# Attention beside a mixture of experts: nine attention steps per block instead of eleven, and a rule for which two may share a gap

## The chip, the cores and the metric

The kernel runs on one core of a Trainium2 chip. Its time is the device time of one execution in microseconds (us); smaller is better. The time before is the median of three executions, 1349.92 us (1348.86 to 1350.81).

## What is computed

Both halves read the layer norm of the same input, and their results are added to the input. The input has 8 sequences of 1024 tokens, each token 256 wide; everything is float32.

```python
def attn(x):                                   # 16 heads of 16
    q, k, v = (x @ W.T for W in (Wq, Wk, Wv))  # split into heads
    q, k = elu(q) + 1, elu(k) + 1
    kv_cumsum = cumsum(einsum('blhd,blhe->blhde', k, v), axis=1)
    k_cumsum = cumsum(k, axis=1)
    out = einsum('blhd,blhde->blhe', q, kv_cumsum)
    denom = clip(einsum('blhd,blhd->blh', q, k_cumsum), 1e-6)
    return (out / denom) @ Wo.T

def ffn(x):                                    # 8 experts, best 2 per token
    c = softmax of the two largest of (x @ Wr + br), zero elsewhere
    h = silu(x @ W1[e]) * (x @ W3[e])          # 256 -> 512
    return sum over e of c[e] * (h @ W2[e])    # 512 -> 256

xn = layernorm(x)
return x + attn(xn) + ffn(xn)
```

## The kernel before

**Two kinds of work share the engines.** The experts' part is cut into tiles of 128 tokens that go to one expert: `NM` = 132 tiles, run by the loop over `j` (L1268). One tile is `ffn_step(j)` (L1237): it gathers the tokens of tile j + 3, loads the two weight matrices of tile j + 2 (1 MB, L1182), multiplies tile j by them (`ffn_hidden`, tile `gu_ps`, two PSUM banks, L1199), turns the tokens of tile j + 1 (`ffn_turn`, tile `xg_t`), multiplies the hidden values of tile j - 1 by the third matrix (`ffn_out`, tile `y_ps`, L1218) and stores finished rows by a scattering DMA that adds (`ffn_store`, L1229).

The attention is cut into `NBLK` = 16 blocks of 512 tokens, and a block into `NCH` = 4 chunks of 128. It is linear attention with a causal mask inside a chunk and a running state `kv` across chunks. A block's work comes in these pieces, to which the text gives letters:

- **Q** (L795) and **K** (L811): projections of queries and keys, four matmul groups in all, each into one bank; ScalarE and VectorE then make elu + 1 of them. **T** (L858): the keys are turned. **V** (L811): the projection of values. **D** (L880): denominators; their reciprocals go through memory and come back as `rden` (L892, L898).
- **S**c, `scores(t, c)` (L909): the products of chunk c into **four banks** `s_ps` (L919); VectorE multiplies each bank by the causal mask into `s_sb` (L926). Then the chunk's part of the state, `kv_ps` (L934), which VectorE adds to `kv` (L939, L941).
- **W**c, `weigh` (L945): state times queries (L953) and masked scores times values (L960) into `o_ps`; VectorE multiplies by `rden` into `oT` (L967).
- **A**c, `attend` (L972): `oT` times the output weights into `a_ps` (L979); ScalarE copies it to `at` (L984), and a DMA on GpSimd's queue adds `at` to the output after the fourth chunk (L989; in the last block after each chunk, L987).

**PSUM.** There are eight banks in three pools. Pool `mm` has four: Q, K and V take one for each group, `gu_ps` takes two, and S takes all four. Pool `y` has two (`y_ps`, `a_ps`, `den`), and pool `t` has two (`xg_t`, `kv_ps`, `o_ps` and the turned keys).

**Order.** A Python generator, `block_steps(t)` (L993), yields once per step; a block has 11. Before each tile, the loop calls `attend_upto(n)` (L1021) with a quota n, and that many steps in total are then issued ahead of the tile. The text calls the place between two tiles a gap. From `j` = 22 (`READ`) on, 148 steps are spread over 106 gaps, 1.4 to a gap, so that about four gaps in ten hold two steps, whichever two they happen to be. Up to `j` = 11 a step comes every other gap; from 12 to 21, where VectorE also builds the second list of tokens, two come in each.

After the opening part the order in each engine's queue is not that of the program: a scheduler places instructions by a model of when their operands and buffers will be ready, and takes the earlier in the program where several are. DMAs on SyncE's queue keep the program's order among themselves.

Of the kernel before, what the change touches and what calls it, by code (L numbers as in the profile page):

```python
# [63 lines left out]
def tile_attention_moe(  # L64
# [20 lines left out]
    NCH = TB // P  # L85
    N = B * L
    NBLK = N // TB
# [821 lines left out]
    def scores(t, c):  # L909

        qT, qm, kT, kn, va, rden = blocks[t]
        first = t % BLK_PER_SEQ == 0 and c == 0
        last = t % BLK_PER_SEQ == BLK_PER_SEQ - 1 and c == NCH - 1
        span = bass.ts(c, P)
        s_ps = [ps_mm.tile([P, KC, 2, P], F32, tag="mm", name="s_ps") for r in range(4)]
        for hh in range(KC):
            for r in range(4):
                rows = slice(32 * r, 32 * r + 32)
                nc.tensor.matmul(  # L919
                    s_ps[r][:, hh].rearrange("p a l -> p (a l)"), lhsT=kT[rows, hh, span],  # L920
                    rhs=qm[rows, hh, :, span], start=True, stop=True,
                )
        s_sb = []
        for r in range(4):
            sm = masked.tile([P, KC * 2, P], F32, tag="s_sb", name="s_sb")
            nc.vector.tensor_tensor(  # L926
                sm, s_ps[r].rearrange("p k a l -> p (k a) l"), causal_b, ALU.mult
            )
            s_sb.append(sm)
        before_c = state[0]  # L930
        if not last:
            kv_ps = ps_t.tile([P, KC, P], F32, tag="t", name="kv_ps")
            for hh in range(KC):
                nc.tensor.matmul(  # L934
                    kv_ps[:, hh, :], lhsT=kn[:, c, bass.ts(hh, P)],
                    rhs=own_v(va, c, 4 * hh, 4 * hh + 4), start=True, stop=True,
                )
            new = three.tile([P, KC, P], F32, tag="kv", name="kv")
            nc.vector.tensor_tensor(new, kv_ps, heads_b, ALU.mult)  # L939
            if not first:  # L940
                nc.vector.tensor_tensor(new, new, before_c, ALU.add)  # L941
            state[0] = new
        return t, c, s_sb, before_c
# [28 lines left out]
    def attend(t, c, oT):  # L972
# [17 lines left out]
        if c == NCH - 1:  # L990
            del ats[t], blocks[t]

    def block_steps(t):  # L993

        for i, _ in enumerate(project(t)):
            if i in (1, 3, 5, 8):
                yield
        if t + 1 < NBLK:
            fetch(t + 1)
        waiting = scores(t, 0)  # L1000
        yield
        for c in range(NCH):
            coming = scores(t, c + 1) if c + 1 < NCH else None
            oT = weigh(*waiting)
            yield
            attend(t, c, oT)
            if c in (0, 2):
                yield
            waiting = coming

    STEPS = 11
    steps_made = [0]

    def attention():
        for t in range(NBLK):
            yield from block_steps(t)

    steps = attention()
    copied = []

    def attend_upto(n):  # L1021
        while steps_made[0] < min(n, NBLK * STEPS):
            next(steps)
            steps_made[0] += 1
        if steps_made[0] == NBLK * STEPS:
            next(steps, None)


    EN = mybir.EngineType
    with tc.manual_schedule(engines={EN.DVE, EN.Activation, EN.PE, EN.Pool}):  # L1030
        parts = [moments(t, 1) for t in range(FB)]
        lgT4 = e_one.tile([P, FB, P], F32, name="lgT4")
        small_constants()
        next(parts[0])
        qs = [project_q(0, o) for o in range(KC)]
        for t in range(FB):
            if t + 1 < FB:
                next(parts[t + 1])
            next(parts[t])
            normalise(t)  # L1040
            turn(t)
            if t == 1:
                logits(0, lgT4[:, 0, :])
            elif t == 0:
                xnTs[0] = turned_first.pop()
                begin(0)
            if t < KC:
                next(qs[t])
        last_moments = moments(FB, 1)
        next(last_moments)  # L1050
        for t in range(1, FB):
            logits(t, lgT4[:, t, :])
        for _ in last_moments:
            pass
        lg4 = ps_t.tile([P, FB * P], F32, tag="t", name="lg4")
        for t in range(FB):
            nc.tensor.transpose(lg4[:, bass.ts(t, P)], lgT4[:, t, :], ident)
        store(FB - 1)
        add_logits(0, FB, lg4)
        for q in qs:  # L1060
            next(q)
        normalise(FB)
        ks = [project_k(0, c) for c in range(0, NCH, 2)]
        routing = route(0, FB)
        next(routing)
        next(ks[0])
        next(routing)
        turn(FB)
        next(ks[1])
        for q in qs:  # L1070
            next(q)
        next(routing)
        listing = first_batch()
        next(listing)
        next(routing)
        lg_t = logits_turned(FB)
        vs = [project_v(0, c) for c in range(0, NCH, 2)]
        next(vs[0])
        next(listing)
        next(vs[0])  # L1080
        next(listing)
        add_logits(FB, 1, lg_t)
        next(listing)
        for o in range(KC):
            mask_q(0, o)
        next(vs[1])
        for k in ks:
            next(k)
        for _ in moments(FB + 1, 1):
            pass  # L1090
        next(vs[1])
        attend_upto(3)

        for _ in range(2):
            idle_ps = ps_mm.tile([P, TB], F32, tag="mm", name="idle_ps")
            nc.tensor.matmul(
                idle_ps, lhsT=ident, rhs=blocks[0][0][:, 0, :], start=True, stop=True
            )
        next(routing)

        nc.scalar.activation(warm, ones[:, 0:1], AF.Silu)
# [135 lines left out]
    def ffn_step(j, behind):  # L1237


        if j + 3 < NM:  # L1240
            ffn_load(j + 3)
        if j + 2 < NM:
            ffn_weights(j + 2)
        if j < NM:
            ffn_hidden(j, j == NM - 1)
        if j + 1 < NM:
            ffn_turn(j + 1)
        if j > 0 and j != NM - 1:
            ffn_out(j - 1)
        for _ in range(2):  # L1250
            if stored[0] < j - behind:
                ffn_store(stored[0])
                stored[0] += 1
# [10 lines left out]
    LATE = 3  # L1264
    LISTS = NBLK - FB
    READ = LISTS + 10
    AHEAD = 2 + LISTS // 2 + 2 * (READ - LISTS)
    for j in range(NM + 1):  # L1268
        if j + 1 < NM:
            ffn_norm(j + 1)  # L1270
        t = FB + j
        if FB < t <= NBLK and t % ROUND == 0:
            for _ in routing:
                pass
        if 0 < j and t < NBLK:
            if j % 2 == 0:
                with tc.issue_after(last_token[0].ins):
                    for _ in moments(t, 2):
                        pass
            normalise(t)  # L1280
            turn(t)
            if t + 5 < NBLK:
                load_x(t + 5, nc.scalar)
            add_logits(t, 1, logits_turned(t))
            if (t + 1) % ROUND == 0:
                routing = route(t + 1 - ROUND, t + 1)
                next(routing)
        if j == LISTS:
            in_order(
                nc.sync.dma_start(  # L1290
                    out=tab_d[1][1 : 1 + NS * P, :].rearrange("(p i) w -> p (i w)", p=P),
                    in_=tab.rearrange("p i w -> p (i w)"),
                )
            )
            in_order(nc.sync.dma_start(out=tab_d[1][0:1, :], in_=before[0:1, 0:3]))
            lists = second_batch(taken)
        if LISTS <= j < READ:
            next(lists)
        if LISTS <= j < LISTS + NBLK - FB:
            t = FB + j - LISTS  # L1300
            rows = slice(t * TB, (t + 1) * TB)
            in_order(nc.sync.dma_start(out=out_rows[rows, :], in_=x_rows[rows, :]))
        if j < LISTS:
            attend_upto(3 + j // 2)
        elif j < READ:
            attend_upto(AHEAD - 2 * (READ - j - 1))
        else:
            attend_upto(AHEAD + (NBLK * STEPS - AHEAD) * (j - READ + 1) // (NM - READ - 4))
        if j == N1 + 1:
            copied.append(j)  # L1310
            in_order(nc.sync.dma_start(out=out_rows[0 : FT * P, :], in_=acc_d[:, :]))
        ffn_step(j, LATE if N1 < j <= N1 + LATE else 0)
    while stored[0] < NM:
        ffn_store(stored[0])
        stored[0] += 1
# [50 lines left out]
```

## Time and profile before

| | |
|---|---|
| median of the timed runs | 1349.92 us |
| the profiled execution | 1333.92 us |
| its span, first to last instruction | 1332.0 us |
| TensorE's mean granted clock | 0.992 |
| PE busy | 1279.3 us, 96% |
| PE weight loads busy | 1094.5 us, 82% |
| VectorE, ScalarE, GpSimd busy | 48%, 39%, 40% |
| DMA, over the span | 187 GB/s |

The profiled execution took 16.0 us less than the median of the timed ones. All sums below are made against the profiled execution. Matmuls overlap in the profile: a row's duration runs beyond the start of the next row. How long a group held TensorE is therefore read from its start to the start of the next group. Each float32 matmul stands as two records, so that `gu_ps` has 32 records for a tile.

### The profile page before, as it was taken

To read this page: it belongs to the slowest core of one execution; us is meant where nothing else is said; L and a number is where in the kernel's file an instruction comes from. 1 tells how busy PE (TensorE), PEld (TensorE's weight loads), DVE (VectorE), ACT (ScalarE), POOL (GpSimd) and SP (SyncE) were. 2 spreads that over 40 slices of the span, in tenths; PEclk is the share of its full clock that TensorE was granted. 3 is DMA by queue.
4 is the path that set the end of the run, shared out by engine and by line. 5 is a ranking of instruction groups with operands and counts; after the bars stand their busy time and mean duration, and the time that the engine had idled before them with its cause. 6 is when DMAs were issued, how large, how long until landed. Compare 5 with 4: busy or idle time off the path is not lost.

```text
span 1332.0 us, 28306 instructions
## 1 busy us (share of the span) xinstructions
PE 1279.3 (96%) x10968; PEld 1094.5 (82%) x10968; DVE 635.0 (48%) x1436; ACT 516.5 (39%) x1052; POOL 528.2 (40%) x460
## 2 busy tenths in 40 slices
PE   5799999999999999999999999999999999999996
PEld 4578787878888788888888888888888888888885
DVE  7867498753353425353443535253533534252531
ACT  4666373531515142342516152432425151524321
POOL 3634433333334334344344434344344343343432
PEclk9999999999999999999999999999999999999998
DMA  9898756566776667576666766675766676576663
GB/s 339 276 297 238 201 162 180 127 179 174 205 201 169 173 142 204 134 195 166 151 188 144 201 164 178 160 195 146 176 165 150 176 175 183 144 198 148 179 163 76
DMA packets 163462, 240.36 MB, mean 180 GB/s; under 512 B 16098, under 2 KB 87394, under 8 KB 163042
## 3 DMA queue, kind: packets, MB, share of 16 engines
q1 hardware_dynamic: 119938, 184.31, 44.4%
q0 software_dynamic: 38064, 43.22, 20.1%
q10 hardware_dynamic: 5328, 11.01, 2.3%
q8 instruction: 90, 1.47, 0.4%
q14 instruction: 42, 0.34, 0.1%
HBM read 196.30 MB, written 52.67 MB: 187 GB/s over the span
## 4 chain that ended last, share of the span: by engine, by line
PE 86%; DVE 8%; DMA 3%; SPq 1%; issue 1%; ACT 1%; POOL 0%; POOLq 0%; DVEq 0%; ACTq 0%
PE gu_ps L1199 35%; PE y_ps L1218 16%; PE s_ps L919 6%; PE o_ps L960 4%; PE a_ps L979 4%; PE zq L795 4%; PE zkk L811 4%; PE zkv L811 3%; PE xg_t L1166 2%; PE kv_ps L934 2%; DVE s_sb L926 2%; PE o_ps L953 2%; DMA xb<-in_x_dram 2%; DVE ksum L863 1%; DMA acc_d<-in_x_dram 1%
## 5 line engine op out<-in xcount | busy, mean ns | idle before, releaser
L1199 PE MATMUL gu_ps<-xgT,w 128*128 128x128 f32 x4224 | 512.4, 278 | 4.6 <-DVE s_sb L926 2.8
L1199 PEld LDWEIGHTS gu_ps<-xgT,w 128*128 128x128 f32 x4224 | 492.3, 192 | 29.4 <-issue 15.7
L1145 POOL DMA_INDIRECT xg<-in_x_dram,src_i x132 | 131.9, 999 | 451.9 <-ACT xgT L1168 361.2
L1218 PE MATMUL y_ps<-w_sb,hT 128*128 x1056 | 251.8, 381 | 2.8 <-DVE hT L1210 2.5
L1229 POOL DMA_INDIRECT out_dram<-y,dst_i x107 | 173.8, 1624 | 164.8 <-DVE y L1225 71.5
L1210 DVE TENSOR_TENSOR hT<-gu_ps,hT 128x512 f32<-128x512 f32 x132 | 91.1, 690 | 272.0 <-PE gu_ps L1199 254.5
L1218 PEld LDWEIGHTS y_ps<-w_sb,hT 128*128 128x128 f32 x1056 | 190.7, 191 | 25.5 <-DVE hT L1210 2.7
L1207 ACT ACTIVATE hT<-gu_ps 128x512 f32<-128x512 f32 x132 | 78.8, 597 | 334.9 <-PE gu_ps L1199 332.7
L926 DVE TENSOR_TENSOR s_sb<-s_ps,causal 128x512 f32<-128x512 f32 x256 | 162.7, 682 | 52.6 <-PE s_ps L919 49.8
L1225 DVE TENSOR_SCALAR y<-y_ps,entry 128x256 f32<-128x256 f32 x132 | 63.6, 482 | 145.3 <-PE y_ps L1218 145.2
L1150 POOL DMA_INDIRECT entry<-tab_d,of_i x107 | 110.0, 1028 | 36.8 <-issue 31.7
L1168 ACT COPY xgT<-xg_t 128x256 f32<-128x256 f32 x132 | 49.1, 372 | 157.8 <-PE xg_t L1166 152.6
L919 PE MATMUL s_ps<-qm,kT 32*128 32x256 f32 x1024 | 95.4, 406 | 1.4 <-DVE hT L1210 0.4
L984 ACT COPY at<-a_ps 128x256 f32<-128x256 f32 x64 | 23.8, 371 | 170.7 <-PE a_ps L979 170.7
L919 PEld LDWEIGHTS s_ps<-qm,kT 32*128 32x128 f32 x1024 | 55.9, 183 | 31.2 <-issue 18.5
L1157 ACT ACTIVATE xg<-xg,entry 128x256 f32<-128x256 f32 x132 | 79.7, 603 | 3.6 <-DVE v L286 3.2
L1229 POOL DMA_INDIRECT acc_d<-y,src_i x25 | 43.5, 1742 | 76.9 <-DVE y L1225 47.4
L979 PE MATMUL a_ps<-wo_sb,oT 128*128 128x256 f32 x256 | 67.6, 386 | 5.6 <-DVE oT L967 5.4
L960 PE MATMUL o_ps<-s_sb,va 128*32 128x128 f32 x2048 | 72.3, 278 | 0.0
L960 PEld LDWEIGHTS o_ps<-s_sb,va 128*32 128x32 f32 x2048 | 53.2, 110 | 9.2 <-issue 0.9
L795 PE MATMUL zq<-xnT,wq_sb 128*128 128x512 f32 x128 | 60.2, 603 | 0.0
L979 PEld LDWEIGHTS a_ps<-wo_sb,oT 128*128 128x128 f32 x256 | 46.2, 190 | 16.8 <-DVE oT L967 9.7
(211 smaller groups left out, 1363.5 us busy)
## 6 DMA issues: line engine op xcount, KB each, us to landing
w<-in_w_dram SPq DMA_DIRECT2D x264, 512.0 KB
den_d<-over SPq DMA_DIRECT2D x64, 128.0 KB
rden<-den_d SPq DMA_DIRECT2D x16, 512.0 KB
xnT_d<-xnT ACTq DMA_DIRECT2D x15, 512.0 KB
xnT<-xnT_d SPq DMA_DIRECT2D x15, 512.0 KB
out_dram<-in_x_dram SPq DMA_DIRECT2D x12, 512.0 KB
out_dram<-at POOLq DMA_DIRECT2D x12, 512.0 KB, 8.2
xb<-in_x_dram SPq DMA_DIRECT2D x10, 512.0 KB
```

What stands on the lines that cost most here:

```text
L795: nc.tensor.matmul(z, lhsT=wq_sb[:, k, bass.ts(o, P)], rhs=xnTs[t][:, k, :], start=(k == 0), stop=(k == KC - 1),)
L811: nc.tensor.matmul(z[:, i, :], lhsT=xnTs[t][:, k, bass.ts(c + i, P)], rhs=wkv_sb[:, k, a, :], start=(k == 0), stop=(k == KC - 1),)
L919: nc.tensor.matmul(s_ps[r][:, hh].rearrange("p a l -> p (a l)"), lhsT=kT[rows, hh, span], rhs=qm[rows, hh, :, span], start=True, stop=True,)
L926: nc.vector.tensor_tensor(sm, s_ps[r].rearrange("p k a l -> p (k a) l"), causal_b, ALU.mult)
L960: nc.tensor.matmul(o_ps[32 * r : 32 * r + 32, hh, :], lhsT=va[:, c, 4 * hh + r, a, :], rhs=s_sb[r][:, 2 * hh + a, :], start=(first and a = ...
L979: nc.tensor.matmul(a_ps, lhsT=oT[:, hh, :], rhs=wo_sb[:, hh, :], start=(hh == 0), stop=(hh == 1),)
L1145: nc.gpsimd.indirect_dma_start(out=xg[j], out_offset=None, in_=x_rows[:, :], in_offset=bass.IndirectOffsetOnAxis(ap=src_i[:, i : i + 1], a ...
L1150: nc.gpsimd.indirect_dma_start(out=entry[j], out_offset=None, in_=table[:, :], in_offset=bass.IndirectOffsetOnAxis(ap=num_i[:, i : i + 1], ...
L1199: done = nc.tensor.matmul(ps[:, i, :], lhsT=w13[:, k, bass.ts(i, P)], rhs=xgT[j][:, k, :], start=(k == 0), stop=(k == KC - 1),)
L1210: nc.vector.tensor_tensor(hT, gu[1], hT, ALU.mult)
L1218: done = nc.tensor.matmul(y_ps, lhsT=hT[:, i, :], rhs=w2_sb[:, bass.ds(e * (IC * H) + i * H, H)], start=(i == 0), stop=(i == IC - 1),)
L1229: nc.gpsimd.indirect_dma_start(out=rows[:, :], out_offset=bass.IndirectOffsetOnAxis(ap=dst_i[:, i : i + 1], axis=0), in_=ys.pop(j), in_off ...
```

## The change

A block now has nine steps. **A**c is no longer a step of its own: it is issued in a later step, behind the next chunk's scores. `attend_upto` gets a rule: a second (or third) step joins a gap only if its number in the block is 0, 4 or 8; otherwise it waits for the next gap, even if the quota is not met. The call in the opening part is exempt.

| step | before | after |
|---|---|---|
| 0 | A3 of the block before, Q | Q, A3 of the block before |
| 1 | K | K |
| 2 | T | T |
| 3 | V, D | V, D |
| 4 | S0 | S0 |
| 5 | S1, W0 | S1, W0 |
| 6 | A0 | S2, A0, W1 |
| 7 | S2, W1 | S3, A1, W2 |
| 8 | A1, S3, W2 | W3, A2 (in the last block A3 too) |
| 9 | A2 | |
| 10 | W3 | |

```diff
+    behind = []
+
     def block_steps(t):
 
+
         for i, _ in enumerate(project(t)):
+            if i == 1 and behind:
+                attend(*behind.pop())
             if i in (1, 3, 5, 8):
                 yield
         if t + 1 < NBLK:
             fetch(t + 1)
         waiting = scores(t, 0)
         yield
+        done = None
         for c in range(NCH):
             coming = scores(t, c + 1) if c + 1 < NCH else None
+            if done and c + 1 < NCH:
+                attend(*done)
             oT = weigh(*waiting)
+            if done and c + 1 == NCH:
+                attend(*done)
+            done = t, c, oT
+            waiting = coming
+            if c + 1 < NCH or t + 1 < NBLK:
+                yield
+        behind.append(done)
+        if t + 1 == NBLK:
+            attend(*behind.pop())
             yield
-            attend(t, c, oT)
-            if c in (0, 2):
-                yield
-            waiting = coming
-
-    STEPS = 11
+
+    STEPS = 9
+
+    TOGETHER = (0, 4, 8)
     steps_made = [0]
...
-    def attend_upto(n):
+    def attend_upto(n, apart=True):
+        first = True
         while steps_made[0] < min(n, NBLK * STEPS):
+            if apart and not first and steps_made[0] % STEPS not in TOGETHER:
+                break
             next(steps)
             steps_made[0] += 1
-        if steps_made[0] == NBLK * STEPS:
-            next(steps, None)
+            first = False
...
-        attend_upto(3)
+        attend_upto(3, False)
...
-    AHEAD = 2 + LISTS // 2 + 2 * (READ - LISTS)
+    AHEAD = 2 + LISTS // 2 + 3 * (READ - LISTS) // 2
...
-            attend_upto(AHEAD - 2 * (READ - j - 1))
+            attend_upto(AHEAD - 3 * (READ - j - 1) // 2)
         else:
             attend_upto(AHEAD + (NBLK * STEPS - AHEAD) * (j - READ + 1) // (NM - READ - 4))
...
+    assert steps_made[0] == NBLK * STEPS
```

`AHEAD` falls from 28 of 176 steps to 23 of 144, and from `j` = 22 on 121 steps are spread over the same 106 gaps.

## The prediction

> **What bounds the kernel now.** I read the page first (busy shares, chain of waits), then the stages, then the timelines of PE and VectorE gap by gap.
>
> ```profile
> PE 1279.3 (96%) x10968; PEld 1094.5 (82%) x10968; DVE 635.0 (48%) x1436; ACT 516.5 (39%) x1052; POOL 528.2 (40%) x460
> ...
> PE 86%; DVE 8%; DMA 3%; SPq 1%; issue 1%; ACT 1%; POOL 0%; POOLq 0%; DVEq 0%; ACTq 0%
> ```
>
> The chain runs through PE for 86% of the span; no other engine is half busy. So the time is PE's work plus the time in which PE waits, and a change of order can win only the second. The stages say where:
>
> ```profile
> 360.00:1289.00 929.00, 921.28 (x7999) 797.17 (x7994) 387.42 (x687) 326.77 (x606) 377.77 (x311) 1.00 0.66 170
> ```
>
> (Columns: window, length, busy PE, weight loads, VectorE, ScalarE, GpSimd, then clock, DMA share, GB/s.) In this long stage PE looks 99% busy, at full clock, with DMA at 0.66. Waits inside a run of matmuls don't show there; the timeline has them. Two gaps, the first with S0 and then S1, W0, the second with S2, W1 (rows: start, length, line, what, records):
>
> ```profile
> 364.16 1.89 PE L1218 MATMUL y_ps<-w_sb,hT 128*128 x8
> 365.98 1.15 PE L919 MATMUL s_ps<-qm,kT 32*128 32x256 f32 x16
> 367.05 0.71 PE L934 MATMUL kv_ps<-va,kn 128*128 128x128 f32 x4
> 367.89 2.92 PE L919 MATMUL s_ps<-qm,kT 32*128 32x256 f32 x16
> 370.74 0.71 PE L934 MATMUL kv_ps<-va,kn 128*128 128x128 f32 x4
> ...
> 384.93 1.15 PE L919 MATMUL s_ps<-qm,kT 32*128 32x256 f32 x16
> 386.01 0.71 PE L934 MATMUL kv_ps<-va,kn 128*128 128x128 f32 x4
> 386.56 0.61 PE L953 MATMUL o_ps<-qT,kv 128*128 128x128 f32 x4
> 387.10 1.08 PE L960 MATMUL o_ps<-s_sb,va 128*32 128x128 f32 x32
> ```
>
> From start to next start, S takes 1.08 us alone (384.93 to 386.01), but 2.85 as the second S of a gap (367.89 to 370.74). VectorE's timeline has the cause: the four masks of the first S take 2.48 us, and each frees one of the four banks that the second S wants.
>
> ```profile
> 367.14 2.48 DVE L926 TENSOR_TENSOR s_sb<-s_ps,causal 128x512 f32<-128x512 f32 x4 [0.57 <-PE s_ps L919]
> ...
> 370.43 1.89 DVE L926 TENSOR_TENSOR s_sb<-s_ps,causal 128x512 f32<-128x512 f32 x3
> 372.23 0.41 DVE L939 TENSOR_TENSOR kv<-kv_ps,heads 128x256 f32<-128x256 f32 x1
> 372.68 0.42 DVE L941 TENSOR_TENSOR kv<-kv 128x256 f32<-128x256 f32 x1
> 373.02 0.68 DVE L926 TENSOR_TENSOR s_sb<-s_ps,causal 128x512 f32<-128x512 f32 x1
> ```
>
> A second kind of wait is an A placed before its `oT` is made:
>
> ```profile
> 601.86 0.71 PE L919 MATMUL s_ps<-qm,kT 32*128 32x256 f32 x6
> 602.83 1.13 PE L979 MATMUL a_ps<-wo_sb,oT 128*128 128x256 f32 x4 [0.27 <-DVE oT L967]
> 603.89 1.12 PE L919 MATMUL s_ps<-qm,kT 32*128 32x256 f32 x10
> ```
>
> **What the Trainium skill says.** (1) "Perfetto Trace Analysis", section Identifying the Most-Contended Engine: matmul busy share is no measure of PE's headroom, because matmuls are pipelined. The trace agrees: 99% busy in a stage whose gaps hold 39 us of waiting (below). (2) The same page, section Matmuls: independent groups should rotate through PSUM banks so that emptying one overlaps the next group. Two S on the same four banks cannot; the trace shows 1.77 us for it. (3) "TensorE: Matmul & The Clock Gate", section Step-by-step: matmuls stay in program order, only weight loads are pulled ahead. So W, A and the tile behind a waiting S wait too; at 367.89 nothing overtakes.
>
> **The price list.** Undisturbed paces, start to next start, from the same timeline: a tile 5.52 us (`gu_ps` 3.57, `xg_t` 0.22, `y_ps` 1.73), S 1.08, kv 0.55, W 1.01 plus 0.54 for its state part, A 0.86, Q 3.43, K and V 3.46, T 0.87, D 0.57. For each of the 100 gaps from 360 to 1295 us I take tile start to tile start less these. The sum is 39.2 us of waiting, by what shares the gap:
>
> - S0 with S1 W0, four gaps, 2.3 each: 9.2
> - S2 W1 with A1 S3 W2, four, 2.0 each: 8.0
> - A0 with S2 W1 where `oT` is late, two at 1.36; A inside the next `gu_ps` before its `oT`, four at 0.4 to 1.0: 5.6
> - T with V D, six at 0.5 to 0.64: 3.6
> - V D with S0, four at 0.49: 2.0. S0 alone, five at 0.53 (the next `gu_ps` needs a bank that is being masked): 2.7
> - the other 77, about 0.1 each: 8.0
>
> **After the change, stage from 360 us.** I ran the new quota and rule by hand over j. In blocks 3 to 15 every gap holds one step, except V D with S0 (8 times), S3 A1 W2 with W3 A2 (5), W3 A2 with Q (2).
>
> - No gap has two S, and none has T with V: 9.2 + 8.0 + 3.6 go.
> - A0 stands behind S2, A1 behind S3, A2 behind W3, A3 behind Q. In the late case above `oT` is done at 602.78, and an S and kv begun at 601.86 last until 603.49, so no wait is left: the 5.6 go.
> - V D with S0: 8 x 0.49 = 3.9. S0 alone 5 x 0.53 = 2.7. V D alone 5 x 0.1 = 0.5.
> - S with W in one gap, 34 gaps outside the pairs, at the 0.17 to 0.30 of today's such gaps, mean 0.22: 7.5. Q 1.4 and W3 A2 1.0 at 0.11; K and T none.
> - S3 A1 W2 with W3 A2: not in the trace. W3 needs the fourth mask of S3, which needs W2's end, because seven `s_sb` buffers serve eight. Nearest row: W ends at 372.84, that mask at 373.70; W3's state part covers 0.54, so 0.3 to 0.4 is left. Bounds: 0 if the scheduler puts W3 into the next `gu_ps`; 1.2 if VectorE makes `oT` and adds `kv` (0.41 + 0.42) first. I take 0.4, and 0.22 as before: 5 x 0.6 = 3.0.
>
> Sum 20.0; 39.2 - 20.0 = 19.2, taken as **18** for the small terms that a scheduler moves.
>
> **Up to 360 us.** To j = 7 nothing changes. From j = 8 to 24 (124 to 360 us) I count 28 us of waiting, much of it behind VectorE, which is 13.46 of 14 us busy in one gap with the token lists. Clear collisions: S1, S2 and S3 close together at 222 to 233 us, 2.8; S0 with S1 W0 at 282 to 295 us, 4.9, in which the clock falls (0.87 in that window; the Trainium skill, "TensorE: Matmul & The Clock Gate", section What's actually happening, ties half clock to an idle window, and PE waits much in this one). Both go. Against that, S2 A0 W1 comes to j = 8, where A0 alone stood, about 1; and j = 18 gets three steps at once (S3 A1 W2, W3 A2, Q), 1 to 2. Bounds: no gain, or 10. I take **5**.
>
> **Edits at nothing.** Q and K never share a gap now, so ScalarE loads its table (1283 ns) up to twice more in some blocks; ScalarE is 39% busy and `gu_ps` covers it with 3.57 us; uncovered, it would be 1.3 a time. A3 comes 3.4 us later, and with it the DMA of `at` on GpSimd's queue and the gather behind it: gathers are three tiles ahead. Once, at j = 26, SyncE's copy from `acc_d` waits for that DMA (8.5 us today) with weight loads behind it; two tiles of weights are ahead, so 3.4 more is covered; uncovered it costs 3.4 once. The assertion and the exemption in the opening issue nothing.
>
> **The end.** In the last block A1, A2 and A3 now come together at j = 127, so three `at` DMAs, not two, go ahead of the last stores on GpSimd, which follow each other at 4.5 to 5.3 us there. One more is some 3 us, of which the tiles take up most: I add **1** (0 to 3).
>
> **Sum.** 18 + 5 - 1 = 22 us of the profiled 1333.92, so about 1312 there. The timed median is 16.0 us higher for a reason that the profile doesn't show; I carry it unchanged: 1349.9 - 22 = **1328**. About 0.2% (2.7 us) is what a measurement of this kernel can tell from no change.
>
> **Rivals.**
> - *The collisions go, the early stage gives nothing or a little back* (1334): VectorE's list work sets the pace from 167 to 282 us, and moved steps just wait elsewhere. Against it: the wait at 282 us has VectorE half idle. 18 - 1 - 1 = 16.
> - *More goes* (1317): early 10, V D with S0 hidden better, no half-clock window; 33 us at most.
> - *The other side: A in the middle of S.* The queue is the scheduler's, not the program's. If it judges `oT` ready midway through S2 and S3, the pattern at 601.86 (1.16 us: 0.57 + 0.20 + 0.39, where S, A and S wait) comes back in up to three gaps of each of 13 blocks: 39 x 1.16 = 45, less 22: 1373. It decides from 19 such gaps of 39 on. For it: the pattern is in the trace. Against: there A came first in the program, and S overtook it; now S comes first.
> - *It doesn't do what it says*: the scheduler moves a step's S into the neighbouring gap, so that two meet again. If half the collisions of S stay, 9 come back: 1337. In the trace S stays within its gap from 360 us on.
>
> **How the numbers follow.** Forecast 0.47; early stage gives nothing 0.14; more goes 0.08; half the collisions stay 0.08; A in the middle, weak (within 2.7 us of no change) 0.06 and decisive 0.17. Hence faster 0.77, same 0.06, slower 0.17. The range 1315 to 1349 takes in the first four cases, with the unknown costs (pairs 0 to 6, early 0 to 10, end 0 to 3), and part of the weak one; about 0.2 lies outside.
>
> **What would show it.** PE's busy time nearly as before; S at 1.08 in every gap after 360 us; no wait of A for `oT`; VectorE's share unchanged in us; VD with S0 still at 0.5. Wrong if the chain turns to VectorE's `s_sb` or `oT`, or if waits of `gu_ps` for `w` appear: tiles that follow each other faster need 1 MB each 5.5 us, which the trace shows served only at the end.

## The result and the profile after

| | median, us | lowest to highest |
|---|---|---|
| before, timed beside the change | 1350.37 | 1348.86 to 1351.32 |
| after | 1329.04 | 1325.97 to 1330.46 |

The ratio is 0.9838, with an interval of 0.9819 to 0.9857: 21.3 us less. The forecast was 1328, 22 us less.

The profiled execution of the changed kernel took 1329.68 us, close to its median. The one of before that the prediction worked from took 1333.92, 16 us under its own median. A later execution of the unchanged kernel took 1352.62 (span 1350.8), like the timed runs; the experiments call it *before again*. After is read against that one here, though it is the slowest of its twelve executions (median 1351.1). Busy shares and chain of waits, first of before again:

```profile
PE 1288.5 (95%) x10968; PEld 1099.8 (81%) x10968; DVE 636.9 (47%) x1436; ACT 516.1 (38%) x1052; POOL 527.7 (39%) x460
...
PE 87%; DVE 8%; issue 2%; DMA 1%; ACT 1%; another core or an unknown queue 1%; POOL 0%; POOLq 0%; DVEq 0%; ACTq 0%
```

Then of after:

```profile
PE 1270.6 (96%) x10968; PEld 1092.2 (82%) x10968; DVE 636.9 (48%) x1436; ACT 526.1 (40%) x1060; POOL 523.1 (39%) x460
...
PE 87%; DVE 7%; ACT 2%; issue 1%; DMA 1%; another core or an unknown queue 1%; POOL 0%; POOLq 0%; DVEq 0%; ACTq 0%
```

PE and VectorE execute the same number of instructions; VectorE's busy time is the same to 0.1 us, so no work went. PE's busy time falls by 17.9 us because a matmul record that waits for its bank counts as busy, and so does one that runs at a lower clock (below). ScalarE gains eight instructions and 10.0 us: eight loads of its table at the 1.28 us that the prediction gave for one. The chain still runs through PE, and ScalarE's share of it rises from 1% to 2%.

The new step with S2, A0 and W1 looks like this in the first profile after (timeline of PE; start, length, line, what, records):

```profile
466.58 1.15 PE L919 MATMUL s_ps<-qm,kT 32*128 32x256 f32 x16
467.65 0.71 PE L934 MATMUL kv_ps<-va,kn 128*128 128x128 f32 x4
468.20 1.03 PE L979 MATMUL a_ps<-wo_sb,oT 128*128 128x256 f32 x4
469.07 0.61 PE L953 MATMUL o_ps<-qT,kv 128*128 128x128 f32 x4
469.61 1.08 PE L960 MATMUL o_ps<-s_sb,va 128*32 128x128 f32 x32
470.62 3.84 PE L1216 MATMUL gu_ps<-xgT,w 128*128 128x128 f32 x32
```

From start to start S takes 1.07 us, kv 0.55, A 0.87, the state part of W 0.54, the rest of W 1.01. These are the undisturbed paces of the prediction's list: none of these groups waits, and the whole gap, tile included, holds 0.19 us of waiting. The second S of a gap used to take 2.85.

**Where the time came from.** I cut both executions at three places: the start of tile 6 (all that is ahead is the opening, which the change leaves alone), the end of the stage in which VectorE builds the second list (to the point where Q, K and T of block 3 are issued in both; where one order has also issued V and D by then, 4.1 us are taken out), and the start of the last tile. In the late stage I add up waits as the prediction did, from tile start to tile start less the undisturbed paces, up to the start of the fourth tile from the end.

| us | before again | after | after, a second time |
|---|---|---|---|
| opening, to the start of tile 6 | 116.7 | 117.6 | 118.4 |
| list stage, same work | 250.7 | 249.0 | 250.8 |
| late stage, waits | 47.1 | 25.4 | 23.2 |
| start of the last tile to the end | 19.2 | 18.9 | 18.8 |
| span | 1350.8 | 1328.0 | 1328.2 |

For the first pair the differences are +0.9, -1.7, -21.7 and -0.3, together the -22.8 of the span. For the second, +1.7, +0.1, -23.9 and -0.4 make -22.5 of -22.6. So the gain lies in the late stage. It holds these waits (number of gaps or pairs in brackets):

| late stage, us | before, as predicted from | before again | after | after, a second time |
|---|---|---|---|---|
| two S in a gap | 17.2 (8) | 20.3 (8) | 0 | 0 |
| A ahead of its `oT` | 5.6 (6) | 6.4 (7) | 0 | 0.9 (1) |
| T with V D | 3.6 | 3.6 | 0 | 0 |
| V D with S0 | 1.9 (4) | 1.9 (4) | 8.2 (8) | 5.3 (8) |
| S0 alone | 2.7 (5) | 2.7 (5) | 2.7 (5) | 2.7 (5) |
| S3 A1 W2 with W3 A2 | none | none | 5.0 (5) | 5.0 (5) |
| the rest | 8.1 | 12.2 | 9.5 | 9.3 |
| sum | 39.2 | 47.1 | 25.4 | 23.2 |

Not all of the 47.1 is waiting that the change removes. In before again TensorE's granted clock stood at 0.50 from about 1049.4 to 1056.2 us, as this window inside that stretch shows (columns as in the prediction, the clock third from the end):

```profile
1050.00:1053.00 3.00, 3.00 (x37) 2.32 (x36) 2.17 (x5) 0.00 (x0) 0.00 (x0) 0.50 1.10 304
```

The gap there (S0 with S1 W0) cost 4.0 us instead of the 2.3 that the same gap cost in the first profile, and the tile behind it, whose `gu_ps` took 5.12 us instead of 3.67, cost 1.5 instead of 0.1. So 3.2 us of the 47.1 came with the half clock: 1.7 of it stands in the row of two S, 1.5 in the rest. Neither profile of the change has a half clock between 370 and 1300 us. With this set aside the late stage gained 18.5 and 20.7 us. Whether the waiting in that gap lowered the clock or the lower clock only met it there, no run shows. The timed runs don't owe their gain to it: in the third set below the mean granted clock was 0.9883 before and 0.9888 after, and from these two figures I estimate the clock's part at 1 us of the 22.6 there.

The view of the stage as a whole, before again and then after, shows little of this, since PE looks 99% busy in both, at a clock that is rounded to 1.00:

```profile
371.50:1331.00 959.50, 948.62 (x8164) 821.12 (x8161) 393.68 (x695) 332.12 (x617) 386.60 (x316) 1.00 0.64 168
```

```profile
366.60:1309.00 942.40, 937.06 (x8196) 818.87 (x8195) 398.04 (x701) 343.03 (x630) 386.28 (x319) 1.00 0.67 173
```

About the same number of matmuls (8164 and 8196 in the windows) takes 17.1 us less.

### The profile page after: what moved, and what is told of

It reads as the page before. It is cut to its first block, busy times and chain, and to the rows that moved or that the text cites. A ratio compares the mean times of both kernels' runs of the same rounds, so it can differ in the third digit from the quotient of the medians.

```text
span 1328.0 us, 28290 instructions
## 1 busy us (share of the span) xinstructions
PE 1270.6 (96%) x10968; PEld 1092.2 (82%) x10968; DVE 636.9 (48%) x1436; ACT 526.1 (40%) x1060; POOL 523.1 (39%) x460
## 4 chain that ended last, share of the span: by engine, by line
PE 87%; DVE 7%; ACT 2%; issue 1%; DMA 1%; another core or an unknown queue 1%; POOL 0%; POOLq 0%; DVEq 0%; ACTq 0%
PE gu_ps L1216 34%; PE y_ps L1235 16%; PE o_ps L960 5%; PE s_ps L919 5%; PE a_ps L979 4%; PE zq L795 4%; PE zkk L811 4%; PE zkv L811 4%; PE kv_ps L934 2%; PE o_ps L953 2%; PE xg_t L1183 2%; DVE s_sb L926 1%; PE tp L333 1%; PE den L880 1%; PE tp L858 1%
## 5 line engine op out<-in xcount | busy, mean ns | idle before, releaser
L1162 POOL DMA_INDIRECT xg<-in_x_dram,src_i x132 | 128.1, 970 | 406.1 <-ACT xgT L1185 322.4
L1167 POOL DMA_INDIRECT entry<-tab_d,of_i x107 | 106.5, 995 | 32.6 <-issue 30.5
L919 PE MATMUL s_ps<-qm,kT 32*128 32x256 f32 x1024 | 85.5, 405 | 0.5 <-DVE hT L1227 0.4
L919 PEld LDWEIGHTS s_ps<-qm,kT 32*128 32x128 f32 x1024 | 51.0, 184 | 24.2 <-issue 19.6
L811 PE MATMUL zkk<-wkv_sb,xnT 128*128 128x256 f32 x256 | 60.0, 384 | 0.0
```

Source lines behind the costliest of these rows:

```text
L811: nc.tensor.matmul(z[:, i, :], lhsT=xnTs[t][:, k, bass.ts(c + i, P)], rhs=wkv_sb[:, k, a, :], start=(k == 0), stop=(k == KC - 1),)
L919: nc.tensor.matmul(s_ps[r][:, hh].rearrange("p a l -> p (a l)"), lhsT=kT[rows, hh, span], rhs=qm[rows, hh, :, span], start=True, stop=True,)
L1162: nc.gpsimd.indirect_dma_start(out=xg[j], out_offset=None, in_=x_rows[:, :], in_offset=bass.IndirectOffsetOnAxis(ap=src_i[:, i : i + 1], a ...
L1167: nc.gpsimd.indirect_dma_start(out=entry[j], out_offset=None, in_=table[:, :], in_offset=bass.IndirectOffsetOnAxis(ap=num_i[:, i : i + 1], ...
```

## The experiments

Theory: the time is the waits in the gaps, above all two S in one gap, and the fold of A and the rule remove them both. Rivals: the rule alone does it, or the fold alone does it; the list stage holds a part of the gain, or none. Three sets ran, each beside the kernel before. The first and third ran on one chip, called chip one here, where before took 1350.62 and 1349.99 us; the second ran on another, chip two, where before took 1337.37 (1335.22 to 1339.03).

**1. The kernel before, unchanged** (`before_again`), to see whether the 16 us between the profiled execution and the timed ones is chance.

> The kernel before, profiled once more. The profile shown of before (1333.9 us) was 16 us under its timed runs, the profile after (1329.7 us) is like its own. Theory: the shown profile of before is a quick specimen, and the 16 us lie in the opening (before 117 us, in the loads), where the change touches nothing: this profile takes 1350, 10 us or more of the difference before the seventh tile, and its stage from tile 29 on is within 3 us of that of the first profile. Rival: the 16 us lie in the collisions themselves, whose size varies: then the stage from 360 us on is some 10 us longer than in the first profile.

Measured: 1351.1 us, ratio 1.0001 (0.9992 to 1.001), profiled span 1350.8. All eight two-S gaps are there again and cost 20.3 us instead of 17.2: 1.7 of it is the half clock, the other 1.5 lies in the four gaps of S2 W1 with A1 S3 W2, in which A stands in the middle of S3. One of them, timeline of PE, then VectorE's rows of the same stretch:

```profile
473.87 0.71 PE L919 MATMUL s_ps<-qm,kT 32*128 32x256 f32 x6
475.87 1.13 PE L979 MATMUL a_ps<-wo_sb,oT 128*128 128x256 f32 x4 [1.30 <-DVE oT L967]
476.93 1.13 PE L919 MATMUL s_ps<-qm,kT 32*128 32x256 f32 x10
...
474.80 0.69 DVE L926 TENSOR_TENSOR s_sb<-s_ps,causal 128x512 f32<-128x512 f32 x1 [0.27 <-PE o_ps L960]
475.40 0.41 DVE L967 TENSOR_TENSOR oT<-rden,o_ps 128x256 f32<-128x256 f32 x1
```

S stops after six of its 16 records, A waits 1.30 us for an `oT` that VectorE makes only after a mask, and the other ten records of S stand behind A. In the same gap of the first profile A waited 0.94:

```profile
463.95 1.13 PE L979 MATMUL a_ps<-wo_sb,oT 128*128 128x256 f32 x4 [0.94 <-DVE oT L967]
```

(The gap of the prediction's example, with a wait of 0.27, cost 1.35 us in both.) Six more gaps, with A inside Q or inside a tile, cost 0.3 to 0.5 us more each. So before again has somewhat more of the same waits. By stages it was longer by 6.7 us in the opening (start of tile 6 at 116.7 instead of 110.1), 4.6 in the list stage (250.7 instead of 246.1) and 8.1 in the late stage, and shorter by 0.5 at the end. Of the 4.6, 3.4 are one gap, from 288.3 us on, in which the clock stood at 0.50 for 10.2 us instead of 3.4; of the 8.1, 3.2 came with the half clock above. About a third of the difference is thus the clock of these two executions.

**2. The fold without the rule** (`nine_no_rule`):

```diff
-    def attend_upto(n, apart=True):
+    def attend_upto(n, apart=False):
```

> The change without the rule on which steps may share a gap. By hand, from tile 22 on there are 15 gaps with two steps as with the rule, of which 3 hold two S (none with the rule) but only 2 hold V D with S0 (8 with it). Theory (the fold to nine steps does most, since it takes the pairs from 42 to 15): 1327 to 1333, within 4 us of the change. Rival (the rule does most): 1338 or more, half of the gain lost.

Measured: 1341.5 us, ratio 0.9932 (0.9918 to 0.9946). It is a miss: the fold alone gives 9 us, and the rule is worth some 12 to 14. They are not where I looked for them. In the late stage the waits are 28.3 us, only 2.9 over the change, with two S in three gaps (5.7) and a half clock of 3.4 us from 906 us on. The list stage takes 257.0, 8.0 more than in the change and 6.2 more than in its second profile, and the opening 1.1 more. Timeline of the gap with S1 W0 and S2 W1 in the list stage, VectorE's rows after those of PE:

```profile
231.18 1.96 PE L919 MATMUL s_ps<-qm,kT 32*128 32x256 f32 x16
233.07 0.71 PE L934 MATMUL kv_ps<-va,kn 128*128 128x128 f32 x4
236.04 0.71 PE L953 MATMUL o_ps<-qT,kv 128*128 128x128 f32 x4 [2.26 <-DVE kv L939]
...
233.00 0.33 DVE L591 TENSOR_SCALAR parts<-held,row 128x440 bf16<-128x440 bf16 x1
233.25 0.61 DVE L586 TENSOR_TENSOR held<-rows,in_row 128x440 bf16<-128x440 f32 x1
233.77 1.88 DVE L926 TENSOR_TENSOR s_sb<-s_ps,causal 128x512 f32<-128x512 f32 x3
235.57 0.42 DVE L939 TENSOR_TENSOR kv<-kv_ps,heads 128x256 f32<-128x256 f32 x1
```

W1 waits 2.26 us for the state `kv`. Between the matmul of the state at 233.07 and the addition at 235.57, VectorE makes list rows (L591, L586) and three masks. So a second S costs more here, where VectorE has other work in its queue. But this gap, which holds some 7 us of waiting, doesn't explain the 8.0: in the change the same steps stand in two gaps, with 2.9 and 3.3 us. Which gaps of the list stage make up the difference, and why, is open.

**3. The eleven steps, with two S kept apart** (`eleven_apart`), a narrower rule without the fold, made from the kernel before. Steps 5 and 8 may not be second in a gap, and nothing else is barred:

```diff
     def attend_upto(n):
+        first = True
         while steps_made[0] < min(n, NBLK * STEPS):
+            if not first and steps_made[0] % STEPS in (5, 8):
+                break
+            first = False
             next(steps)
             steps_made[0] += 1
```

> The kernel before with one rule only: a second step is not taken into a gap where it would bring a second S (steps 5 and 8). A0, A1, A2, A3 stay where they were. Theory (the collision of S on four banks is the larger part): it takes away about 17 us of waiting after 360 us, and gives 3 to 5 back, since A0 now shares the gap with W0 eight times; 1336 to 1340. Rival (A waiting for oT is the part that counts): 1347 to 1352.

Measured: 1336.56 us, ratio 0.9895 (0.988 to 0.991), as expected: 14.1 of the 21 to 23 us. Late waits are 33.0, or 14.1 less than in before again (3.2 of them the half clock there); no gap holds two S, and gaps with A inside another group now cost 14.5 us. The list stage takes 246.7, which is 4.0 less than in before again, but no less than the 246.1 of the first profile of the same kernel before: the clock stood at 0.50 for 3.4 us of that stage in both of these, and for 10.2 us in before again. So this run shows no gain in the list stage. Timeline of PE:

```profile
459.40 1.60 PE L1203 MATMUL gu_ps<-xgT,w 128*128 128x128 f32 x12
461.50 1.13 PE L979 MATMUL a_ps<-wo_sb,oT 128*128 128x256 f32 x4 [0.49 <-DVE oT L967]
462.47 2.39 PE L1203 MATMUL gu_ps<-xgT,w 128*128 128x128 f32 x20
```

A step of A alone has nothing of the attention ahead of it, so the scheduler sets it into the next tile, and there it waits for `oT` (0.49 us) with the tile behind it: 15 gaps, 8.5 us (the rest of the 14.5 is A inside Q, 3.3, and A in the middle of S, 2.7). This is what the fold removes. The view of tile `a_ps` says the same of the two ends; what the idle time before A (that of its weight loads counted too) ended with, in us and times, over the whole execution, before again and then after:

```profile
  DVE oT L967: 23.0, 29
```

```profile
  DVE oT L967: 0.3, 1
```

Neither part alone gives the gain: 9 us for the fold, 14 for keeping S apart, 21 to 23 for both.

**4. A3 behind S0 rather than in Q** (`a3_behind_s0`, made from the changed kernel):

```diff
         for i, _ in enumerate(project(t)):
-            if i == 1 and behind:
-                attend(*behind.pop())
             if i in (1, 3, 5, 8):
                 yield
...
         waiting = scores(t, 0)
+        if behind:
+            attend(*behind.pop())
         yield
```

> The change, with A3 of the block before issued behind S0 instead of behind Q. After S0 nothing stands between S and the next tile, whose gu_ps wants a bank that is being masked; the profile after shows 0.5 us for it where S0 is alone and 0.5 to 1.4 us where V D is ahead of it. A3 (0.86 us) would stand there. Theory: 13 blocks at 0.5 to 0.9 us, so 6 to 11 us less than the change: 1318 to 1323. Rival (gu_ps waits for VectorE however long, and A3 is put elsewhere by the scheduler): 1327 to 1331.

Measured: 1323.1 us, ratio 0.9797 (0.9784 to 0.9811): 5.9 us under the median of the change, which was timed in another set, and at the upper edge of what was expected. Late waits fall to 17.1, with V D and S0 at 2.4 instead of 8.2 or 5.3, and S0 alone at 1.0 instead of 2.7. Timeline of PE:

```profile
449.09 1.36 PE L919 MATMUL s_ps<-qm,kT 32*128 32x256 f32 x16
450.38 0.71 PE L934 MATMUL kv_ps<-va,kn 128*128 128x128 f32 x4
450.93 1.03 PE L979 MATMUL a_ps<-wo_sb,oT 128*128 128x256 f32 x4
451.80 3.80 PE L1216 MATMUL gu_ps<-xgT,w 128*128 128x128 f32 x32
```

A3 takes 0.87 us of PE that it took elsewhere anyway, and while it runs VectorE masks the bank that the tile's `gu_ps` wants; the tile then runs its 32 records without a stop.

**5. Fewer steps in the list stage** (second set, on chip two). First one step in each of the ten gaps (`early_one`), then none (`early_none`):

```diff
-    AHEAD = 2 + LISTS // 2 + 3 * (READ - LISTS) // 2
+    AHEAD = 2 + LISTS // 2 + (READ - LISTS)
...
-            attend_upto(AHEAD - 3 * (READ - j - 1) // 2)
+            attend_upto(AHEAD - (READ - j - 1))
```

```diff
-    AHEAD = 2 + LISTS // 2 + 3 * (READ - LISTS) // 2
+    AHEAD = 2 + LISTS // 2 + 1
...
-            attend_upto(AHEAD - 3 * (READ - j - 1) // 2)
+            attend_upto(AHEAD)
```

> The change with fewer attention steps while the second list is built: one step a gap from tile 12 to 21 (18 steps by tile 21, not 23), the rest spread over the later gaps. Theory (in that stage VectorE makes the list and the masks of S, and matmuls of S wait for masks that stand behind list work; fewer S there, less waiting): 3 to 7 us less in the stage, 2 to 3 given back by five more pairs S3 A1 W2 with W3 A2 later: 1323 to 1328. Rival (the stage waits for the list itself, whatever attention does): the work moved out comes back later in full, 1330 to 1336.

> The change with no attention step between tile 13 and 21. Theory of competing masks: VectorE's list work (four times 1.6 us and the tile's 1.2 us, so some 7.7 us a gap, from the rows of 167 to 282 us) is then longer than TensorE's own work in a gap (5.5 us for the tile, 0.8 for the list), so TensorE waits some 1.4 us in each of eight gaps, and attention that could have filled them comes later: 1330 to 1340. If TensorE waits for nothing but collisions with attention, the stage empties of waits: 1318 to 1324.

Measured: 1323.38 us, ratio 0.9901 (0.9886 to 0.9916), and 1332.95, ratio 0.9975 (0.9959 to 0.999). Both lie in ranges that their expectations gave, but those were made for a chip on which before takes 1350 us; by the ratio the two gain 13 and 3 us of before's 1337. They stand on the same chip, so the 9.6 us between them count. The stage without steps, as windows:

```profile
177.00:246.00 69.00, 56.10 (x393) 47.60 (x391) 59.09 (x151) 35.03 (x148) 32.21 (x22) 0.95 0.60 183
```

VectorE is busy for 59.09 of 69 us and PE for 56.10. Waits in these gaps reach 6.3 us, mostly for list rows that VectorE makes:

```profile
200.60 0.76 PE L725 MATMUL held_ps<-parts,at_place 128*128 128x220 bf16 x4 [2.11 <-DVE parts L591]
```

So without attention steps this stage waits for VectorE, and the steps, which would have filled PE meanwhile, must be done later.

Two more of this set build on experiment 4: S3 A1 W2 and W3 A2 kept apart (`a3_pair_apart`), and the same with one step per list gap (`a3_early_one`, which has the edit of `early_one` besides):

```diff
-    TOGETHER = (0, 4, 8)
+    TOGETHER = (0, 4)
```

> A3 behind S0, and in addition W3 A2 no longer joins S3 A1 W2 in a gap (steps that may join: 0 and 4); W3 A2 with Q takes its place. The pair cost 0.5 to 0.7 us more than its two steps apart in the profile after (W3 split into pieces while it waits for the last mask), W3 A2 with Q 0.2. Theory: five pairs at 0.3 to 0.6, so 1 to 3 us less than with A3 behind S0 alone: 1320 to 1322. Rival (one block later in the early stage, nothing there): 1323.

> The same, with one step a gap from tile 12 to 21 as well. If what early_one gains there adds to the late gain: 3 to 6 us under the run with W3 A2 apart, 1315 to 1318. If the moved steps only move their waits: 1320 to 1326.

Measured: 1317.63 us, ratio 0.9858 (0.9843 to 0.9874), and 1314.34, ratio 0.9833 (0.9819 to 0.9846). The figures in us lie at or under what was expected, but before was 13 us quicker on this chip; by the ratio both gain less than expected. The change itself did not run on chip two.

**6. The same kernels on chip one** (third set: the change itself as `after_again`, and `early_one`, `a3_behind_s0` and `a3_early_one` without any further edit).

> The change once more, on one chip with the variants. The kernel before took 1350.6 us on one chip and 1337.4 on another, and the profile shown of before (1333.9) is like the second: the 16 us between it and its timed runs are then the chip. Theory: the waits of S and A are what differs from chip to chip, so the change gains less where before is quicker: 14 us (ratio 0.990) on a chip like the second, 21 (0.984) on one like the first. Rival: the gain is 0.984 on either.

> One attention step a gap from tile 12 to 21, now beside the change itself on one chip. If list work and masks compete in that stage: 2 to 5 us less than the change. If the moved steps bring their waits along: within 1.5 us of it.

> A3 behind S0, beside the change on one chip. The first profile showed 8.8 us less waiting after 360 us and the time fell by 5.9: 5 to 9 us less than the change here too.

> All three edits (A3 behind S0, W3 A2 not joining S3 A1 W2, one step a gap from tile 12 to 21), beside the change on one chip: 9 to 13 us less than the change, and the fastest of all.

| kernel | us | ratio | interval |
|---|---|---|---|
| the change | 1327.37 | 0.9832 | 0.9815 to 0.985 |
| one step per list gap | 1332.99 | 0.9868 | 0.9844 to 0.9892 |
| A3 behind S0 | 1319.66 | 0.9784 | 0.976 to 0.9809 |
| A3 behind S0, pair apart, one step per list gap | 1320.74 | 0.9784 | 0.9766 to 0.9801 |

The change repeats. One step per list gap is no better than the change: the medians stand 5.6 us the other way, though the intervals touch, where 2 to 5 us less was the hope. In the profiles its list stage, at the same work and less the tiles that run beside it, took 247.8 us against 250.8 and 249.0; late waits give 2.7 of that back (25.9 against 23.2), and its opening, which the edit leaves alone, took 121.1 against 118.4. The two profiles of the change differ by 1.8 in the list stage themselves, so a gain there isn't shown. The two kernels that ran on both chips gain more on chip one (0.9868 against 0.9901, and 0.9784 against 0.9833), where the kernel before has more to lose. Whether the change would also gain less on chip two follows from these two only by likeness. A3 behind S0 is the best version found on chip one: 6 to 8 us under the change in two sets. Keeping the pair apart and thinning the list stage add nothing to it there; 9 to 13 us under the change and the fastest of all were expected, and 6.6 came. The profiles show where it went. With all three edits late waits fall to 14.0 us, 3.0 less than with A3 behind S0 alone, but from the start of the last tile to the end it takes 24.2 us instead of 19.0. Last DMAs of `at` on GpSimd's queue, first with A3 behind S0, then with all three edits:

```profile
1277.82 2.71 POOL L987 DMA_DIRECT2D out_dram<-at  x3 [2.79 <-ACT at L984]
```

```profile
1284.03 1.81 POOL L987 DMA_DIRECT2D out_dram<-at  x2 [4.54 <-DMA out_dram<-y,dst_i]
```

Where W3 A2 A3 of the last block may not join S3 A1 W2, two of the three DMAs come behind one more store of a tile. The last store then starts at 1310.21 us in the one and 1310.55 in the other, though the last tile starts 5.2 us earlier in the second. With the pair apart the end takes 23.8 to 24.2 us in three profiles, on both chips, and 18.8 to 19.4 in every other variant. So the kernel with all three edits loses at the end what it gains before. A rule that spares the last block was not run.

## Why the prediction was right, point by point

**Late stage, 18 us: right in kind, and measured 22 and 24, or 18.5 and 20.7 without the half clock.** The rows that were to go went, but for one gap: two S, A ahead of `oT`, T with V D. From the first profile they were 26.4 us; in before again they are 30.3, and the rest is 4.1 larger too (12.2 against 8.1). Of these 8.0, 3.2 came with the half clock. On the other side the waits after the change were put at 20.0 and are 25.4 and 23.2, so what was left over was underrated by 3 to 5 us. (The prediction's list gives the small ones as 77 gaps; the gaps named before it leave 71 of the 100. Their 8.0 us is right.) Two terms were too small:

- *V D with S0*, 8 x 0.49 = 3.9: measured 8.2 and 5.3. The 0.49 came from four gaps that all looked alike. Two of the gaps after the change, PE's rows first and then VectorE's, in each:

```profile
449.83 0.65 PE L880 MATMUL den<-ksum,own_of 128*32 128x128 f32 x16
450.40 1.36 PE L919 MATMUL s_ps<-qm,kT 32*128 32x256 f32 x16
451.69 0.71 PE L934 MATMUL kv_ps<-va,kn 128*128 128x128 f32 x4
452.42 3.84 PE L1216 MATMUL gu_ps<-xgT,w 128*128 128x128 f32 x32
...
450.54 0.29 DVE L886 TENSOR_SCALAR over<-den 128x128 f32<-128x128 f32 x1 [3.57 <-PE den L880]
451.74 2.42 DVE L926 TENSOR_TENSOR s_sb<-s_ps,causal 128x512 f32<-128x512 f32 x4
```

```profile
522.76 0.64 PE L880 MATMUL den<-ksum,own_of 128*32 128x128 f32 x16
523.33 1.36 PE L919 MATMUL s_ps<-qm,kT 32*128 32x256 f32 x16
524.62 0.71 PE L934 MATMUL kv_ps<-va,kn 128*128 128x128 f32 x4
525.96 3.84 PE L1216 MATMUL gu_ps<-xgT,w 128*128 128x128 f32 x32 [0.63 <-DVE s_sb L926]
...
524.08 0.29 DVE L886 TENSOR_SCALAR over<-den 128x128 f32<-128x128 f32 x1 [4.18 <-PE den L880]
525.27 2.42 DVE L926 TENSOR_TENSOR s_sb<-s_ps,causal 128x512 f32<-128x512 f32 x4
```

The denominators start 0.57 us before S0 in both. VectorE is idle and begins on them 0.71 us after their start in the first gap and 1.32 in the second; the reciprocal and then the masks move with it (masks at 1.34 and 1.94 us after the start of S0), and the tile gets its first bank at once in the one and after 0.63 us of waiting in the other. In the first gap kv to `gu_ps` is 0.73 us, in the second 1.34, where kv alone needs 0.55. In both gaps the view names PE's denominators as what VectorE waited for, and the trace's semaphore events have PE's signal at 450.52 and at 524.06 us, 0.69 and 1.30 us after the group's start: the signal came late, and VectorE followed at once. Why PE signals at different distances isn't in the trace, whose ends of matmuls are modelled. S itself takes 1.29 in these gaps, so "S at 1.08 in every gap" held only where no V D stands ahead of it.

- *S3 A1 W2 with W3 A2*, 5 x 0.6 = 3.0, bounds 0 to 6: measured 5.0 both times. Timeline of PE in such a pair, then VectorE's row of the fourth mask:

```profile
699.18 1.08 PE L960 MATMUL o_ps<-s_sb,va 128*32 128x128 f32 x32
700.19 0.71 PE L953 MATMUL o_ps<-qT,kv 128*128 128x128 f32 x4
700.83 0.42 PE L960 MATMUL o_ps<-s_sb,va 128*32 128x128 f32 x6
701.18 0.49 PE L1216 MATMUL gu_ps<-xgT,w 128*128 128x128 f32 x2
701.60 1.06 PE L960 MATMUL o_ps<-s_sb,va 128*32 128x128 f32 x26
...
700.75 0.69 DVE L926 TENSOR_TENSOR s_sb<-s_ps,causal 128x512 f32<-128x512 f32 x1 [1.10 <-PE o_ps L960]
```

W2 ends at 700.19, and W3's masked part stops after six records until the fourth mask is made, as predicted; two records of the next tile fill a part of the wait. VectorE starts that mask at 700.75 and ends it at 701.44, 1.25 us after W2 ended, where the nearest row of before gave 0.86.

The term *S with W* and the other small ones, put at 10.4, came out at 9.5 and 9.3, and *S0 alone* at the 2.7 predicted.

**List stage, 5 us: the term that failed.** It was 1.7 in the first profile after and -0.1 in the second. No gap of this stage holds two S any more, so the collisions named at 222 to 233 us and at 282 to 295 are gone. But in the first profile after, gaps 14 to 17 and 19 hold 2.8 to 3.4 us of waiting each, where the first profile of before has 1.2 to 3.2, and S2 A0 W1 at j = 8 cost 3.6 us (with a half clock in that gap) and 2.0, not 1. That is the mechanism of the rival "the early stage gives nothing": VectorE sets the pace there. A window of this stage, after, has it busy for 41.45 of 43 us:

```profile
203.00:246.00 43.00, 39.41 (x344) 30.96 (x345) 41.45 (x107) 17.08 (x69) 15.87 (x11) 1.00 0.60 169
```

Experiment 5 agrees: with no attention steps at all, PE waits there for VectorE's list rows. No run made the list work itself shorter, which would be the direct test. The order of steps isn't without effect, since leaving the rule out of the nine took 6 to 8 us more in this stage.

The low clock at 282 to 295 us, which the prediction let vanish with the collision, did not. In the profile that it worked from, the clock there stood at 0.50 for 3.4 us; in before again for 10.2 (the window below); in each of the two of the change again for 3.4, near 290 us:

```profile
288.00:305.60 17.60, 16.62 (x114) 12.68 (x113) 7.18 (x14) 1.47 (x3) 4.46 (x4) 0.71 0.80 232
```

**The end, 1 us:** it cost nothing (19.2 before again, 18.9 and 18.8 after, from the start of the last tile on).

**The 16.0 us carried unchanged.** They are the difference between that one profile and the timed runs. Most likely the profile was taken on another chip: on chip one no timed run of before came below 1345.3 us. This isn't shown, because it isn't known which chip it ran on, and 1333.92 lies a little under chip two's lowest, 1335.22. Experiment 1 splits the difference to before again into the opening, the list stage and the late stage, about a third of it half clock; the late part is partly of the kind that the change removes. So "unchanged" was wrong by a few us, in the direction that made up for the list stage. That the forecast of 1328 came within 1 us of 1329.04 is luck to that extent: the forecast of 22 was 18 late and 5 early less 1 at the end; 21 to 23 came, nearly all of it late.

**Edits at nothing.** ScalarE's eight more table loads cost nothing that can be seen: Q and K stay among small waits. One wait of A for `oT` is left in the first profile after, 0.3 us in the whole execution. In the second one A0 waited 0.46 us behind S2 and kv (at 471.22), in the one gap of the table with 0.9: there VectorE made `oT` late because `rden` had only just come from memory, which the fold doesn't help. Of the signs that the prediction named, one came out otherwise: PE's busy time did not stay nearly as before but fell by 17.9 us against before again (8.7 against the first profile), since a record that waits counts as busy.

**The rivals.** In both profiles of the change no gap has A in the middle of S, so the case of 1373 had no place, and none has two S. "The early stage gives nothing" was right about the early stage; its 1334 was too high because the late gain was larger than 18 and the end cost nothing.

## What to carry to other kernels

Where an in-order engine is 99% busy, find its waits from start to next start against its undisturbed pace; then place work so that two users of the same banks do not follow each other, and so that a short independent group (here an A behind the next S) stands between a producer and whoever needs its result. In this kernel separating collisions paid in the stage that PE bounds and not in the one in which VectorE is 96% busy: there the waits moved to other gaps, and taking the attention out altogether cost time. Take the profile that a sum is made from, and the time that it is subtracted from, on the same chip, and compare the granted clock stage by stage before a difference between two executions is put down to waits.

## What was not expected of the hardware

- The same program takes 1337.4 us on one chip and 1350.0 to 1350.6 on another, 1% more. The runs on chip two start tile 6 at 111.9 to 113.1 us, those on chip one at 116.7 to 121.1. The cause of this is open.
- The granted clock fell to 0.50 in stretches of 3.4, 6.8 and 10.2 us, at places that differ between executions of one kernel: in the late stage of before again, but not in that of the first profile. This one cost 3.2 us.
- An idle VectorE began on the same operand 0.71 us after the matmuls' start in one gap and 1.32 in another of the same execution, because PE's signal came 0.6 us later, with 0.6 us of waiting for PE behind it.
- A stretch in which PE's records cover 94% of the time (16.62 of 17.60 us) ran at a granted clock of 0.71. Records are longer both while they wait and at half clock, so the busy share tells neither apart, nor which of the two came first.
